# A two-layer graph kernel: self's first product issued inside the last round of left and right, with another order at the head and the end

## The chip, the cores and the metric

The kernel runs on one core of a Trainium2 chip. Times are device microseconds of one execution; the time of a kernel is the median of its runs. TensorE (PE in the profile) multiplies and transposes, VectorE (DVE) and ScalarE (ACT) work element by element and empty PE's banks, GpSimd (POOL) adds and issues stores, SyncE (SP) issues loads. Each engine works through its own queue in order and waits on semaphores of the others. A DMA is issued by an engine's queue and runs on 16 shared DMA engines.

## The reference

Inputs are x (128 graphs of 64 nodes, 768 features), one 64 x 64 adjacency for each graph and the weights of two layers, all in float32.

```python
# layer 0
p = softmax(h @ h.T / sqrt(768)); delta = p * adj
attn = delta / (delta.sum(2) + 1e-10)
ctx = upper(attn) @ (h @ Wl.T + bl) + diag(attn) * (h @ Ws.T + bs) + lower(attn) @ (h @ Wr.T + br)
x = layernorm(x + relu(layernorm(ctx, 1e-12) * gamma + beta))
# layer 1, 12 heads of 64
s = q @ k.T / sqrt(64) + beta * adj, masked where adj == 0
x = layernorm(x + softmax(s) @ v)
```

## The kernel before, in words

The 8192 tokens are worked through in 16 blocks (`NBLK`) of 512 tokens, four tiles of 128 (`T`). In the loop over n, layer 1 of block n runs interleaved with layer 0 of block m = n + 1, so that PE always has a product to issue. One turn of the loop goes through these stages on PE: left and right of block m, self of block m, its context, the values of block n, and q and k of block n in two groups.

**The products.** Left, right and self are 768 x 768 products done by a seven-product scheme (`seven`, numbered 1 to 7 in the order `ORDER` = 1, 2, 6, 5, 7, 4, 3): products 1, 6, 7 and 4 build in one PSUM bank (X), 2, 5 and 3 in another (Y), twice over for two token halves j. From block 3 on (`DEEP`) left and right are one nested scheme (`both_sides`, `nested`): seven rounds of seven products, weights from the DRAM tensor `lr_d` in tiles `wlr`. The next round's products 1 and 2 are issued ahead of a round's products 4 and 3; the last round has none after it, so there 4 follows 7 directly. DVE or ACT empties each bank into `u_deep` or `lr` (`middle` and `final`, L599, L601). Values, q and k use 15 products of 256-wide weights (`products`, L486), whose results DVE or ACT adds to `v` (L976) and `qk` (L1003, L1006). The banks X and Y are two each.

**Hooks.** Each stage calls `hooks.get(place)` before a product. `at(hooks, place, f)` puts work there: `sides` (four transposes into `ps_a`, L745, of the masked attention) at place 13 of the right hooks, `scores` and `weighted` of layer 1, loads, and `finish`. Element-wise work of other stages stands in three queues, `first`, `urgent` and `lazy`, and `step` issues one item after each product. So the order of each engine's instructions is fixed by places and queues when the program is built.

**The head.** Weights are first combined. `prepare1` makes 15 further forms of Wv (into `v_d`), Wq and Wk (`qk_d`): it loads nine pieces (L270, on SP's queue), forms 15 sums on DVE (`SUMS_W`, L303 and L305, one per step) and stores the forms that are multiplied (POOL's queue, L277, L284, L286). Pieces and sums live in a few buffers, `homes` (ten named `h_v`, eleven named `h_qk`), taken from the front of a list and put at its end when their last use is issued. Block 0 to 2 have plain left and right products (`side_part`), since `lr_d` is not ready. `deepened(i)` forms the second-level matrices of `lr_d` for one i: four loads into `w_deep` (four of the twelve buffers of the weight stream `wv`, `wqk`, `wl`), four copies from DRAM to DRAM, eight subtractions on DVE (L388), four stores (L394). A list gives the stage and place of each of the seven.

**The end.** `finish(p, lazy)` normalises block 14 inside the last block's q and k: sums and sums of squares by ACT (L1147, L1150), their variance by DVE (L1123), the root by ACT, the scaled tiles by ACT, stores by POOL. After the last value products come `sixth` parts of the weighted values of the last block (reciprocal and product on DVE, L1392 and L1393, adds on POOL or DVE, L1398), `bn_stats` and `bn_aggr` (L1409, L1412), and the four output tiles, three scaled by ACT and one by DVE, stored by SP (L1424, L1461).

Of the kernel before, what the change touches and what calls it, by code (L numbers as in the profile page):

```python
# [70 lines left out]
def gnn_two_layers(ctx: ExitStack, tc, x, adj, wl, bl, ws, bs, wr, br, gamma, beta,  # L71
# [174 lines left out]
    def prepare1(nm, homes, queue=lazy):  # L246

        w = weights[nm].rearrange("(p c) e -> p c e", c=KC)
        form, key = {}, ("w", nm)
        holder, done = {}, [0]  # L250

        def fresh_form(i):
            home = homes.pop(0)
            holder[i] = home
            return home.rearrange("p (k e) -> p k e", k=2)
# [6 lines left out]
        def loaded(i):  # L262
            if i in form:
                return
            k, j = divmod(i, THIRDS)
            form[i] = raw = fresh_form(i)
            if nm != "v":
                form[i] = raw.rearrange("p k (m e) -> p m k e", m=GROUPS)
            with tc.issue_after(streamed["l"][8] if nm == "k" else streamed["b", "r"].ins) if nm != "q" else ExitStack():
                nc.sync.dma_start(out=raw, in_=w[:, 2 * k : 2 * k + 2, j * TH : (j + 1) * TH])  # L270

# [16 lines left out]
        def summed(i, a, b, op):  # L288
            for _, *pair, _ in SUMS_W[done[0] : done[0] + AHEAD + 1]:
                for x in pair:  # L290
                    if x < THIRDS * THIRDS:
                        loaded(x)
            done[0] += 1
            fresh = [x for x in (a, b) if x < THIRDS * THIRDS and x not in known]
            known.update(fresh)
            form[i] = fresh_form(i)
            if nm != "v":
                form[i] = form[i].rearrange("p m (k e) -> p m k e", k=2)
            with tc.issue_after(recent["u"].ins) if nm == "v" else ExitStack():
                if op == "n":  # L300
                    parts = [form] if nm == "v" else [{k: form[k][:, m] for k in (i, a, b)} for m in range(GROUPS)]
                    for f in parts:
                        nc.vector.scalar_tensor_tensor(f[i], f[a], -1.0, f[b], ALU.mult, ALU.subtract)  # L303
                else:
                    nc.vector.tensor_tensor(form[i], form[a], form[b], ALU.add if op == "+" else ALU.subtract)  # L305
            for x in fresh:
                stored(x)
            stored(i)
            for x in (i, a, b):
                if x in uses:  # L310
                    uses[x] -= x != i
                if not uses.get(x):
                    homes.append(holder.pop(x))

# [212 lines left out]

    def seven(width, factors, first, last, hooks, taps_by_act=False):

# [6 lines left out]
        for k, i in enumerate(ORDER):  # L536
            for j in range(2):
                for f in hooks.get(2 * k + j, ()):
                    f()
                if i == 1:  # L540
                    X[j] = ps_st.tile([P, 512], F32, tag="X", name="ps_X")
                if i in (2, 5):
                    Y[j] = ps_st.tile([P, 512], F32, tag="Y", name="ps_Y")
                ps = (X if i in (1, 6, 7, 4) else Y)[j][:, 0:width]
                fs = factors(i, j)
                for c, (a, b) in enumerate(fs):
# [13 lines left out]
                elif i == 3:  # L560
                    last(j, 0, 1, ps, u[j, 2])
                step(not taps_by_act or (i, j) not in ((5, 1), (7, 0)))

    def by_tokens(nm, S, last, in_sbuf=None, hooks={}):

        wt = dict(in_sbuf or {})

        def factors(i, j):
# [11 lines left out]

        seven(HALF, factors, first, lambda j, m, n, ps, part: last(2 * m + j, n, ps, part), hooks)

# [168 lines left out]
    def self_part(n, in_sbuf, hooks={}):  # L751

        blk = blocks[n]
        o = [x1_p.tile([P, D], F32, tag="x1", name=f"o_{n}_{t}") for t in range(T)]

        def last(t, h, ps, part):
            cols = slice(h * HALF, (h + 1) * HALF)
            recent["u"] = nc.vector.tensor_tensor(o[t][:, cols], ps, bias["s"][:, cols] if part is None else part,
                                                  ALU.add)

        by_tokens("s", blk["S"], last, in_sbuf, hooks)
        blk["x"] = o
# [81 lines left out]
    def context0(n):  # L844
# [5 lines left out]
        if by_act:  # L850
            total, nm, var, std, rstd = (st.tile([P, T], F32, tag=f"c{k}", name=f"c{k}") for k in range(5))

        def unused():
# [57 lines left out]
        def norm(t, mean, rstd):  # L911
            if by_act and (n < NBLK - 1 or t % 2 == 0):
                nc.scalar.activation(o[t], o[t], AF.Identity, bias=nm[:, t : t + 1], scale=rstd)
            else:
                nc.vector.tensor_scalar(o[t], o[t], mean, rstd, ALU.subtract, ALU.mult)
# [7 lines left out]
        def rest(factors):  # L923
            for t, mr in enumerate(factors):
# [3 lines left out]
            fs = [partial(norm, t, *mr) for t, mr in enumerate(mrs)]  # L928
            later(key, *((tiny(partial(lowered, mrs)), *(f if n == NBLK - 1 and t % 2 else act(f) for t, f in enumerate(fs))) if by_act else
                         (lambda: (fs[0](), fs[1]()), lambda: (fs[2](), fs[3]()))))  # L930

# [173 lines left out]
    def finish(n, queue=urgent):  # L1105
# [5 lines left out]
        def sums(fs):  # L1111
            if ends:
                unused = l0t.tile([P, 2, 2, D], F32, tag="lr", name="unused")[:, 0, 0, :]
            else:
                unused = l1s_p.tile([P, T * 6 * L], F32, tag="s", name="unused")[:, 0:D]
            for t in range(T):
# [22 lines left out]

        def act(f):  # L1140
            return f, "root" if ends else "act"

        settle(("y", n, 0))
# [8 lines left out]

        if ends:

            begin = (summed, "after"), GAP, (lambda: (mean(), squared()), "act"), GAP, GAP, tiny(variance), act(root),                 GAP, GAP, GAP, tiny(factors)
        else:
            begin = (summed, "after"), GAP, GAP, tiny(mean), act(squared), GAP, GAP, tiny(variance), act(root), GAP,                 tiny(factors)
        later(key, *begin, *[act(partial(norm, (k, k + 1))) for k in range(0, T, 2)],
# [8 lines left out]
    edges(0)  # L1167
    homes = list(homes_of_v())
    now(loads(0))
# [28 lines left out]
    prep = streams.enter_context(tc.tile_pool(name="prep1", bufs=11))  # L1198
    homes = [prep.tile([P, 2 * TH], F32, tag="h", name="h_qk") for _ in range(11)]
    now(context0(0)[0])  # L1200
# [34 lines left out]
    for n in range(NBLK):  # L1235
# [11 lines left out]

        for i, (when, hooks, place) in zip(ORDER2, ((0, val, 2), (0, val, 8), (0, qk[0], 4), (0, qk[0], 10),
                                                    (0, qk[1], 6), (1, own, 3), (1, val, 3))):
            if when == n:  # L1250
# [8 lines left out]
        if p >= 0:  # L1259
# [141 lines left out]

    def behind(*parts):
        for h, j in parts:
            divided, added = sixth(h, j)
            later(("q", h, j), partial(divided, 0), lambda divided=divided, added=added: (
                divided(1), added(0, nc.gpsimd), added(1, nc.gpsimd)), queue=first)

# [14 lines left out]
    def norm_by_act(t):  # L1422
        nc.scalar.activation(xt[t], xt[t], AF.Identity, bias=shift[:, t], scale=rstd[:, t])
        nc.sync.dma_start(out=out_t[n, t], in_=xt[t])  # L1424

    def early():
# [7 lines left out]
    freed()  # L1434
    divided(0)
    divided(1)
    added(0, nc.gpsimd)
    added(1, nc.vector)
    divided, added = sixth(0, 2)
    for t in (2, 3):  # L1440
        measured(t, 0)
    for t in (0, 1):
        measured(t, 1)
    for t in (3, 2):
        measured(t, 1)
        whole(t)
    factors(slice(2, 4))
    divided(0)
    inverse(slice(2, 4))
    for t in (3, 2):  # L1450
        norm_by_act(t)
    divided(1)
    added(1, nc.gpsimd)
    added(0, nc.vector)
    for t in (0, 1):
        measured(t, 2)
        whole(t)
# [3 lines left out]
    nc.sync.dma_start(out=out_t[n, 0], in_=xt[0])  # L1461
    norm_by_act(1)
# [31 lines left out]
```

## Time and profile before

| | |
|---|---|
| median of 3 runs | 2823.55 us (2822.14 to 2825.18) |
| the profiled execution | 2829.61 us, span 2827.9 us |
| PE busy | 2783.3 us of the span, 17962 instructions |
| DVE, ACT, POOL busy | 1955.9, 1101.6, 958.5 us |
| mean granted clock of PE | 0.997 |
| PE and DVE busy from 100 to 200 us | 95.1 and 81.7 us, DMA share 0.76 |
| PE and DVE busy from 200 to 300 us | 95.1 and 78.9 us, DMA share 0.81 |

In a line of the timeline the columns are start, duration, engine, line of the kernel, operation, tiles written and read, partitions x elements, and how many instructions were drawn together; the bracket gives the idle time before and what ended it. One matmul of the source is two of them.

### The profile page before, as it was taken

The numbers are of one execution on the slowest core, as the hardware profiler recorded it, in microseconds if no ns is written. First come the engines' busy times: TensorE is split into PE (matmuls) and PEld (weight loads), VectorE is DVE, ScalarE is ACT, GpSimd is POOL, SyncE is SP. The second block draws the span as 40 slices with busy tenths as digits, with TensorE's granted clock in tenths as the row PEclk, the third lists the DMA queues.
The fourth block names the chain that finished last, engine by engine and source line by source line (L and its number), as shares of the span: only waits on it lengthen the run. The fifth ranks groups of instructions, "written<-read, shape, count | busy, mean of one in ns | idle before, by whom it ended". The sixth has DMA issues, their size and how long they took to land.

```text
span 2827.9 us, 49388 instructions
## 1 busy us (share of the span) xinstructions
PE 2783.3 (98%) x17962; PEld 2015.5 (71%) x17962; DVE 1955.9 (69%) x3399; ACT 1101.6 (39%) x1907; POOL 958.5 (34%) x1249
## 2 busy tenths in 40 slices
PE   9999999999999999999999999999999999999997
PEld 5558668686776867768577685867768677685786
DVE  5687777677685766767677676776767667676665
ACT  0003324435343452434525344353434534345255
POOL 3244232506134151442415225061341514424121
PEclk9999999999999999999999999999999999999998
DMA  9688595867869587695867858677695876958543
GB/s 345 196 283 271 179 306 171 265 157 232 223 184 272 145 261 193 190 267 152 260 183 211 246 168 264 161 231 226 184 266 147 258 198 192 266 147 260 172 124 98
DMA packets 394847, 604.87 MB, mean 214 GB/s; under 512 B 49296, under 2 KB 277648, under 8 KB 394608
## 3 DMA queue, kind: packets, MB, share of 16 engines
q1 hardware_dynamic: 344624, 502.80, 60.4%
q0 software_dynamic: 18704, 76.89, 7.5%
q10 hardware_dynamic: 31280, 22.03, 4.2%
q8 instruction: 145, 2.38, 0.4%
q14 instruction: 94, 0.77, 0.1%
HBM read 530.00 MB, written 78.45 MB: 215 GB/s over the span
## 4 chain that ended last, share of the span: by engine, by line
PE 87%; DVE 2%; DMA 2%; ACT 1%; issue 0%; DVEq 0%; ACTq 0%; SPq 0%
PE ps_X L486 25%; PE ps_Y L486 17%; PE ps_Y L816 13%; PE ps_X L816 11%; PE ps_X L547 8%; PE ps_Y L547 6%; PE ps_ctx L864 3%; PE sc L1027 2%; PE ps_y L1090 2%; PE u L694 1%; ACT eT L1060 1%; DMA wv<-v_d 0%; DMA sq<-in_x_dram 0%; DMA wlr<-lr_d 0%; DMA ws<-d_s 0%
## 5 line engine op out<-in xcount | busy, mean ns | idle before, releaser
L434 POOL TENSOR_TENSOR sums<-hT 128x768 f32<-128x768 f32 x16 | 28.9, 1808 | 828.2 <-PE ps_X L486 811.3
L1060 ACT ACTIVATE eT<-s 32x384 f32<-32x384 f32 x512 | 266.6, 521 | 44.0 <-DVE s L1043 37.6
L486 PE MATMUL ps_X<-xT,wqk 128*128 128x256 f32 x1024 | 236.2, 381 | 4.9 <-DVE qk L1006 2.5
L875 ACT ACTIVATE unused<-o 128x768 f32<-128x768 f32 x60 | 50.6, 843 | 477.4 <-DMA sq<-in_x_dram 261.1
L486 PEld LDWEIGHTS ps_X<-xT,wqk 128*128 128x128 f32 x1024 | 195.3, 191 | 32.7 <-DVE qk L1006 2.9
L601 DVE TENSOR_TENSOR lr<-ps_Y,u_deep 128x384 f32<-128x384 f32 x273 | 151.8, 556 | 95.8 <-PE ps_Y L816 78.8
L1003 ACT ACTIVATE qk<-ps_X,bq 128x256 f32<-128x256 f32 x128 | 60.6, 473 | 392.9 <-PE ps_X L486 392.7
L816 PE MATMUL ps_Y<-wlr,q 128*128 128x384 f32 x546 | 208.7, 491 | 0.0
L1006 DVE TENSOR_TENSOR qk<-qk,ps_X 128x512 f32<-128x512 f32 x160 | 109.6, 686 | 133.6 <-PE ps_X L486 73.7
L1101 POOL TENSOR_TENSOR o<-o,share 128x192 f32<-128x192 f32 x240 | 135.3, 591 | 145.3 <-DVE share L1098 145.2
L486 PE MATMUL ps_Y<-more,wqk 128*128 128x256 f32 x768 | 181.5, 379 | 0.2 <-DVE qk L1006 0.2
L486 PE MATMUL ps_X<-sums,wqk 128*128 128x256 f32 x768 | 180.3, 381 | 0.4 <-issue 0.4
L547 PE MATMUL ps_X<-ws,hT 128*128 128x384 f32 x540 | 179.4, 486 | 0.3 <-DMA ws<-d_s 0.3
L464 POOL TENSOR_TENSOR more<-xT 128x512 f32<-128x512 f32 x32 | 40.0, 1270 | 381.4 <-DVE xT L422 157.4
L486 PEld LDWEIGHTS ps_Y<-more,wqk 128*128 128x128 f32 x768 | 145.9, 190 | 20.4 <-DVE qk L1006 0.6
L486 PEld LDWEIGHTS ps_X<-sums,wqk 128*128 128x128 f32 x768 | 144.6, 190 | 20.7 <-issue 0.7
L1006 DVE TENSOR_TENSOR qk<-qk,ps_Y 128x512 f32<-128x512 f32 x160 | 108.2, 676 | 69.3 <-PE ps_Y L486 67.2
L601 DVE TENSOR_TENSOR u_deep<-ps_X,lr 128x384 f32<-128x384 f32 x195 | 107.6, 552 | 67.4 <-PE ps_X L816 58.0
L547 PEld LDWEIGHTS ps_X<-ws,hT 128*128 128x128 f32 x540 | 102.4, 190 | 72.0 <-DMA ws<-d_s 1.1
L816 PEld LDWEIGHTS ps_Y<-wlr,q 128*128 128x128 f32 x546 | 101.5, 190 | 67.5 <-DVE lr L601 0.5
L816 PE MATMUL ps_X<-wlr,q 128*128 128x384 f32 x364 | 149.1, 491 | 0.1
L1147 ACT ACTIVATE unused<-o 128x768 f32<-128x768 f32 x60 | 50.6, 844 | 219.2 <-POOL o L1101 216.3
(268 smaller groups left out, 6298.1 us busy)
## 6 DMA issues: line engine op xcount, KB each, us to landing
wlr<-lr_d SPq DMA_DIRECT2D x819, 192.0 KB, 3.6
wqk<-qk_d SPq DMA_DIRECT2D x480, 256.0 KB, 2.6
wv<-v_d SPq DMA_DIRECT2D x240, 256.0 KB, 5.6
ws<-d_s SPq DMA_DIRECT2D x180, 192.0 KB, 6.8
ws<-in_L_gnn_W_self_dram SPq DMA_DIRECT2D x135, 192.0 KB, 3.8
xa<-in_x_dram SPq DMA_DIRECT2D x64, 384.0 KB, 5.7
out_dram<-o POOLq DMA_DIRECT2D x60, 384.0 KB, 7.7
sq<-in_x_dram ACTq DMA_DIRECT2D x56, 384.0 KB, 9.7
```

The source lines that it names most:

```text
L486: nc.tensor.matmul(ps[:, h, :], lhsT=a, rhs=b, start=start and h == 0 and k == 0, stop=k == len(fs[h]) - 1, skip_group_check=True)
L547: nc.tensor.matmul(ps, lhsT=a, rhs=b, start=(c == 0 and i in (1, 2, 5)), stop=(c == len(fs) - 1), skip_group_check=True)
L601: nc.vector.tensor_tensor(dst, view(ps), add, ALU.add)
L816: nc.tensor.matmul(ps, lhsT=a, rhs=b, start=(k == 0 and j in (1, 2, 5)), stop=(k == len(fs) - 1), skip_group_check=True)
L864: nc.tensor.matmul(ps[g * L : (g + 1) * L, 0:HALF], lhsT=blk["aT"][:, t, g * L : (g + 1) * L], rhs=blk["lr"][t][:, g, h * HALF : (h + 1) * ...
L875: nc.scalar.activation(unused(), o[t], AF.Identity, accum_out=total[:, t : t + 1])
L1003: nc.scalar.activation(dst[:, h], ps[:, h, :], AF.Identity, bias=bias["qk"[h]][:, c : c + 1], scale=float(sign))
L1006: nc.vector.tensor_tensor(dst, dst, ps, ALU.add if sign > 0 else ALU.subtract)
L1027: nc.tensor.matmul(sc[t // 2, r][g * L : (g + 1) * L, t % 2, c, :], lhsT=q[rows, c, tok], rhs=k[rows, c, tok], start=True, stop=True)
L1060: nc.scalar.activation(e[to[0], :, to[1]], pairs[rows, :, cols], AF.Exp, scale=1.0 / SCALE)
L1090: nc.tensor.matmul(y[h, r][cols, t, c, :], lhsT=eT[rows, 2 * h + t, c, cols], rhs=by_parity[rows, 2 * h + t, 2 * c + m, g, :], start=True, ...
L1101: nc.gpsimd.tensor_tensor(res, res, share[:, t], ALU.add)
```

## The change

- Self's first product for token half 0 (three matmuls of the source and its three `ws` loads) is issued by `self_begun` at place 13 of the right hooks, right after `sides`, for blocks 3 to 15. Place 13 lies between products 7 and 4 of the last round. `seven` then skips that product in self's own stage and uses the begun bank.
- At the head, raw pieces are loaded by ACT's queue instead of SP's, homes are taken by age of release (with four steps added for a form that is stored), block 0's tiles are normalised by ACT, and the seven `deepened` get other places. Block 1's second `weighted` goes one product later.
- At the end, block 14's moments are taken by DVE's `bn_stats`, two of its tiles are scaled by DVE and two by ACT; the sixths are divided and added at once, all adds by POOL; the last block's tiles 2 and 0 are scaled by DVE, 3 and 1 by ACT.

```diff
         def fresh_form(i):
-            home = homes.pop(0)
-            holder[i] = home
+            home = min(homes, key=lambda h: h[0])
+            homes.remove(home)
+            holder[i] = home = home[1]
             return home.rearrange("p (k e) -> p k e", k=2)
...
-                nc.sync.dma_start(out=raw, in_=w[:, 2 * k : 2 * k + 2, j * TH : (j + 1) * TH])
+                nc.scalar.dma_start(out=raw, in_=w[:, 2 * k : 2 * k + 2, j * TH : (j + 1) * TH])
...
-                    homes.append(holder.pop(x))
+                    homes.append((done[0] + base + (4 if any(u == x for _, u, _, _ in FIFTEEN) else 0), holder.pop(x)))
...
+                ready = i == 1 and j == 0 and begun is not None
                 if i == 1:
-                    X[j] = ps_st.tile([P, 512], F32, tag="X", name="ps_X")
+                    X[j] = begun if ready else ps_st.tile([P, 512], F32, tag="X", name="ps_X")
...
-                fs = factors(i, j)
+                fs = [] if ready else factors(i, j)
...
+    def self_begun(n):
+
+        S = blocks[n]["S"]
+        w = [weight("ws") for _ in range(HC)]
+        ps = ps_st.tile([P, 512], F32, tag="X", name="ps_X")
+        for k in range(HC):
+            nc.sync.dma_start(out=w[k], in_=pieces["s"][1][:, k, :])
+        for k in range(HC):
+            nc.tensor.matmul(ps[:, 0:HALF], lhsT=S[1][:, k, 0:P], rhs=w[k], start=k == 0, stop=k == HC - 1,
+                             skip_group_check=True)
+        blocks[n]["begun"] = w, ps
...
         def norm(t, mean, rstd):
-            if by_act and (n < NBLK - 1 or t % 2 == 0):
+            if n < NBLK - 1 or t % 2 == 0:
...
         if ends:
-
-            begin = (summed, "after"), GAP, (lambda: (mean(), squared()), "act"), GAP, GAP, tiny(variance), act(root),                 GAP, GAP, GAP, tiny(factors)
...
+            mrs = moments(key, xt, 1e-5, queue)
...
+            later(key, tiny(lowered), (partial(by_act, 1), "root"), partial(by_vector, 0), (partial(stored, (0, 1)), "free"),
+                  (partial(by_act, 3), "root"), partial(by_vector, 2), (partial(stored, (2, 3)), "free"), queue=queue)
+            return
...
-        for i, (when, hooks, place) in zip(ORDER2, ((0, val, 2), (0, val, 8), (0, qk[0], 4), (0, qk[0], 10),
-                                                    (0, qk[1], 6), (1, own, 3), (1, val, 3))):
+        for i, (when, hooks, place) in zip(ORDER2, ((0, val, 2), (0, qk[0], 5), (1, left, 8), (1, own, 3),
+                                                    (1, qk[0], 0), (1, qk[0], 7), (1, qk[1], 3))):
...
-                at(right, 0 if m >= DEEP else 1, weighted, p, 1)
+                at(right, 0 if m >= DEEP else 2, weighted, p, 1)
...
                 at(*((left, 11) if m < DEEP else (right, 13)), sides, m)
+                if m >= DEEP:
+                    at(right, 13, self_begun, m)
...
-        at(qk[1], 5 if n == NBLK - 2 else 1, scores, n, 0)
+        at(qk[1], 4 if n == NBLK - 2 else 1, scores, n, 0)
         if last:
-            at(qk[1], 8, finish, p, lazy)
+            at(qk[1], 7, finish, p, lazy)
...
-    def behind(*parts):
...
+    def at_once(*parts):
+        for divided, added in [sixth(h, j) for h, j in parts]:
+            divided(0)
+            divided(1)
+            added(0, nc.gpsimd)
+            added(1, nc.gpsimd)
...
-               11: [partial(behind, (1, 2), (0, 0))], 13: [freed], 14: [early, partial(behind, (0, 1), (1, 0))]}, True)
+               11: [partial(at_once, (1, 2), (0, 0))], 12: [early], 14: [partial(at_once, (0, 1), (1, 0))]}, True)
...
     divided(0)
     divided(1)
     added(0, nc.gpsimd)
-    added(1, nc.vector)
+    added(1, nc.gpsimd)
...
-    for t in (3, 2):
-        norm_by_act(t)
...
+    norm_by_act(3)
+    measured(1, 2)
+    whole(0)
+    whole(1)
     factors(slice(0, 2))
+    norm_by_vector(2)
     inverse(slice(0, 2))
-    nc.vector.tensor_scalar(xt[0], xt[0], mv[:, 0, 0:1], rstd[:, 0], ALU.subtract, ALU.mult)
-    nc.sync.dma_start(out=out_t[n, 0], in_=xt[0])
+    norm_by_vector(0)
     norm_by_act(1)
```

More of the change, by code (lines that the diff above doesn't have):

```diff
@@ L249, in prepare1 @@
         form, key = {}, ("w", nm)
-        holder, done = {}, [0]
+        holder, done, base = {}, [0], len(SUMS_W) * "vqk".index(nm)
         def fresh_form(i):
-            home = homes.pop(0)
-            holder[i] = home
+            home = min(homes, key=lambda h: h[0])
+            homes.remove(home)
+            holder[i] = home = home[1]
             return home.rearrange("p (k e) -> p k e", k=2)
@@ L526, in moments, with seven @@
         return [(mv[:, t, 0:1], rstd[:, t : t + 1]) for t in range(k)]
-    def seven(width, factors, first, last, hooks, taps_by_act=False):
+    def seven(width, factors, first, last, hooks, begun=None):
         X, Y, u = {}, {}, {}
@@ L561, in seven, with by_tokens @@
                     last(j, 0, 1, ps, u[j, 2])
-                step(not taps_by_act or (i, j) not in ((5, 1), (7, 0)))
-    def by_tokens(nm, S, last, in_sbuf=None, hooks={}):
+                step()
+    def by_tokens(nm, S, last, in_sbuf=None, hooks={}, begun=None):
         wt = dict(in_sbuf or {})
+        if begun:
+            wt[1], begun = begun
         def factors(i, j):
@@ L579, in first @@
             return u
-        seven(HALF, factors, first, lambda j, m, n, ps, part: last(2 * m + j, n, ps, part), hooks)
+        seven(HALF, factors, first, lambda j, m, n, ps, part: last(2 * m + j, n, ps, part), hooks, begun)
+    def self_begun(n):
[8 more added lines that the diff above has]
+        blocks[n]["begun"] = w, ps
     def nested(width, sums, load, multiply, view, C, bias0, bias1, hooks):
@@ L759, in last @@
                                                   ALU.add)
-        by_tokens("s", blk["S"], last, in_sbuf, hooks)
+        by_tokens("s", blk["S"], last, in_sbuf, hooks, blk.get("begun"))
         blk["x"] = o
@@ L851, in context0 @@
             total, nm, var, std, rstd = (st.tile([P, T], F32, tag=f"c{k}", name=f"c{k}") for k in range(5))
+        else:
+            nm = st.tile([P, T], F32, tag="c1", name="c1")
         def unused():
@@ L928, in rest @@
             fs = [partial(norm, t, *mr) for t, mr in enumerate(mrs)]
-            later(key, *((tiny(partial(lowered, mrs)), *(f if n == NBLK - 1 and t % 2 else act(f) for t, f in enumerate(fs))) if by_act else
-                         (lambda: (fs[0](), fs[1]()), lambda: (fs[2](), fs[3]()))))
+            later(key, tiny(partial(lowered, mrs)), *(f if n == NBLK - 1 and t % 2 else act(f) for t, f in enumerate(fs)))
         return [partial(part, t) for t in range(T)], (squares, roots, inverse)
@@ L1111, in sums @@
         def sums(fs):
[L1112 to L1115, printed above, removed]
+            unused = l1s_p.tile([P, T * 6 * L], F32, tag="s", name="unused")[:, 0:D]
             for t in range(T):
@@ L1138, in stored @@
                 nc.gpsimd.dma_start(out=out_t[n, t], in_=xt[t])
-        def act(f):
-            return f, "root" if ends else "act"
         settle(("y", n, 0))
@@ L1153, in finish, with lowered, by_vector, by_act @@
         if ends:
-            begin = (summed, "after"), GAP, (lambda: (mean(), squared()), "act"), GAP, GAP, tiny(variance), act(root),                 GAP, GAP, GAP, tiny(factors)
-        else:
-            begin = (summed, "after"), GAP, GAP, tiny(mean), act(squared), GAP, GAP, tiny(variance), act(root), GAP,                 tiny(factors)
+            mrs = moments(key, xt, 1e-5, queue)
+            def lowered():
+                for t in (1, 3):
+                    mean, inverse = mrs[t]
+                    nc.vector.scalar_tensor_tensor(shift[:, t : t + 1], mean, -1.0, inverse, ALU.mult, ALU.mult)
+            def by_vector(t):
+                nc.vector.tensor_scalar(xt[t], xt[t], *mrs[t], ALU.subtract, ALU.mult)
+            def by_act(t):
+                nc.scalar.activation(xt[t], xt[t], AF.Identity, bias=shift[:, t : t + 1], scale=mrs[t][1])
+            later(key, tiny(lowered), (partial(by_act, 1), "root"), partial(by_vector, 0), (partial(stored, (0, 1)), "free"),
+                  (partial(by_act, 3), "root"), partial(by_vector, 2), (partial(stored, (2, 3)), "free"), queue=queue)
+            return
+        begin = (summed, "after"), GAP, GAP, tiny(mean), act(squared), GAP, GAP, tiny(variance), act(root), GAP, tiny(factors)
         later(key, *begin, *[act(partial(norm, (k, k + 1))) for k in range(0, T, 2)],
@@ L1167, in gnn_two_layers @@
     edges(0)
-    homes = list(homes_of_v())
+    homes = [(-1, home) for home in homes_of_v()]
     now(loads(0))
@@ L1198, in gnn_two_layers @@
     prep = streams.enter_context(tc.tile_pool(name="prep1", bufs=11))
-    homes = [prep.tile([P, 2 * TH], F32, tag="h", name="h_qk") for _ in range(11)]
+    homes = [(-1, prep.tile([P, 2 * TH], F32, tag="h", name="h_qk")) for _ in range(11)]
     now(context0(0)[0])
@@ L1400, in sixth @@
         return divided, added
-    def behind(*parts):
[L1403 to L1406, printed above, removed]
+    def at_once(*parts):
[4 more added lines that the diff above has]
+            added(1, nc.gpsimd)
     def measured(t, j):
@@ L1424, in norm_by_act, with norm_by_vector @@
         nc.sync.dma_start(out=out_t[n, t], in_=xt[t])
+    def norm_by_vector(t):
+        nc.vector.tensor_scalar(xt[t], xt[t], mv[:, t, 0:1], rstd[:, t], ALU.subtract, ALU.mult)
+        nc.sync.dma_start(out=out_t[n, t], in_=xt[t])
     def early():
@@ L1430, in gnn_two_layers @@
     values(n, {1: [partial(scores, n, 1, 2, l0t, 7)],
-               11: [partial(behind, (1, 2), (0, 0))], 13: [freed], 14: [early, partial(behind, (0, 1), (1, 0))]}, True)
+               11: [partial(at_once, (1, 2), (0, 0))], 12: [early], 14: [partial(at_once, (0, 1), (1, 0))]}, True)
     settle(("f", n - 1))
     divided, added = sixth(1, 1, ps_st)
-    freed()
+    measured(0, 1)
+    measured(1, 1)
     divided(0)
@@ L1437, in gnn_two_layers @@
     added(0, nc.gpsimd)
-    added(1, nc.vector)
+    added(1, nc.gpsimd)
     divided, added = sixth(0, 2)
+    measured(2, 0)
+    measured(3, 0)
+    divided(0)
+    divided(1)
+    added(0, nc.gpsimd)
+    added(1, nc.gpsimd)
     for t in (2, 3):
-        measured(t, 0)
-    for t in (0, 1):
-        measured(t, 1)
-    for t in (3, 2):
         measured(t, 1)
@@ L1447, in gnn_two_layers @@
     factors(slice(2, 4))
-    divided(0)
+    measured(0, 2)
     inverse(slice(2, 4))
-    for t in (3, 2):
-        norm_by_act(t)
[L1452 to L1457, printed above, removed]
+    norm_by_act(3)
+    measured(1, 2)
+    whole(0)
+    whole(1)
     factors(slice(0, 2))
+    norm_by_vector(2)
     inverse(slice(0, 2))
-    nc.vector.tensor_scalar(xt[0], xt[0], mv[:, 0, 0:1], rstd[:, 0], ALU.subtract, ALU.mult)
-    nc.sync.dma_start(out=out_t[n, 0], in_=xt[0])
+    norm_by_vector(0)
     norm_by_act(1)
```

## The prediction

> **What bounds the kernel now.** I read the page first: its engine table, then its chain.
>
> ```profile
> PE 2783.3 (98%) x17962; PEld 2015.5 (71%) x17962; DVE 1955.9 (69%) x3399; ACT 1101.6 (39%) x1907; POOL 958.5 (34%) x1249
> ...
> PE 87%; DVE 2%; DMA 2%; ACT 1%; issue 0%; DVEq 0%; ACTq 0%; SPq 0%
> ```
>
> TensorE is the bound, idle 2827.9 − 2783.3 = 44.6 us. The change removes no matmul, so it can win only idle time, where the chain leaves PE. I next walked PE's timeline, taking each gap between starts beyond the usual spacing (0.32 us for 384 columns, 0.22 for 256) as lost. A sixth block, PE then DVE:
>
> ```profile
> 1391.54 0.60 PE L745 MATMUL ps_a<-ident,a 128*128 128x128 f32 x4
> 1392.35 1.56 PE L816 MATMUL ps_X<-wlr,sums 128*128 128x384 f32 x4 [0.21 <-DVE u_deep L601]
> 1393.74 1.46 PE L816 MATMUL ps_Y<-wlr,q 128*128 128x384 f32 x4
> 1395.04 3.39 PE L547 MATMUL ps_X<-ws,hT 128*128 128x384 f32 x10
> ...
> 1391.74 0.56 DVE L601 TENSOR_TENSOR u_deep<-ps_X,lr 128x384 f32<-128x384 f32 x1 [1.31 <-PE ps_X L816]
> ```
>
> After product 7 and four transposes, product 4 (1392.35) waits until DVE has emptied product 7's bank. From the last transpose to product 4 it is 0.486 us where 0.109 is usual; the next interval is 0.427 instead of 0.323. Lost: 0.377 + 0.104 = 0.48 us, the same in all 13 blocks that have this round. The head (first 420 us, PE and DVE):
>
> ```profile
> 92.01 2.20 PE L547 MATMUL ps_X<-t_r,hT 128*128 128x384 f32 x6 [1.76 <-DVE u L578]
> ...
> 90.80 0.69 DVE L305 TENSOR_TENSOR h_v<-h_v 128x512 f32<-128x512 f32 x1 [3.35 <-issue]
> ...
> 175.73 2.17 PE L547 MATMUL ps_Y<-wr,hT 128*128 128x384 f32 x6 [2.42 <-issue]
> ...
> 173.78 0.69 DVE L305 TENSOR_TENSOR h_qk<-h_qk 128x512 f32<-128x512 f32 x1 [4.25 <-DMA qk_d<-h_qk]
> ...
> 233.45 1.75 PE L486 MATMUL ps_X<-wv,sums 128*128 128x256 f32 x7 [1.97 <-DMA wv<-v_d]
> ...
> 268.42 1.75 PE L486 MATMUL ps_X<-xT,wqk 128*128 128x256 f32 x7 [2.00 <-DMA wqk<-qk_d]
> ```
>
> Two kinds: DVE, in order, stands before a weight sum whose buffer is still being stored, and evictions queue behind it; or a weight stream is late because one `deepened` holds four of its twelve buffers. The end:
>
> ```profile
> 2775.25 3.34 PE L486 MATMUL ps_X<-xT,wqk 128*128 128x256 f32 x7 [2.46 <-DVE qk L1006]
> ...
> 2774.43 0.17 DVE L1123 TENSOR_SCALAR f<-f 128x4 f32<-128x4 f32 x1 [3.69 <-ACT unused L1150]
> ...
> 2823.48 0.33 SPq L1461 DMA_DIRECT2D out_dram<-o  x1
> 2824.00 0.33 SPq L1424 DMA_DIRECT2D out_dram<-o  x1
> ```
>
> DVE waits 3.69 us for ScalarE's sums of squares while a q/k eviction stands behind; the seven matmuls after it take 3.34 us for 1.75, with a granted clock of 0.5 for 3.4 us.
>
> **The change, part by part.**
>
> *Self's first product.* Three matmuls (six instructions, 6 × 0.323 = 1.94 us) go between the transposes and product 4. They need a bank emptied long before (1388.78 + 0.56), so they start at once, and the eviction that product 4 waits for (it ends at 1392.30) lies under them. Gain 13 × 0.48 = 6.2 us. Their cover: the three `ws` loads keep their place on SP's queue and landed 4.4 to 8.9 us before first use; used 3.07 us earlier, the tightest third load (4.36, used 1.29 us into the product) keeps 2.6 us. Next late is self's second half, which takes the bank of product 4: that is empty 3 × 0.32 + 0.53 + 0.56 + 0.06 = 2.11 us after product 4 starts and wanted after 2.58 us, so 0.47 us remain. DVE's order there is unchanged; product 3's eviction and the ScalarE swaps (12 × 0.86 us) come 1.5 us later, first wanted at 1425.7.
>
> *Head: homes and ScalarE's queue.* Twenty-seven loads of v, q and k pieces leave SP's queue for ScalarE's, where hT copies, exponentials and square roots stand behind them; sums now take the longest-freed buffer. Value sum 14 gets a buffer with no store. Lost at 89.8 and 93.7: 2.03 + 0.54 = 2.6; I take 2.2, as one later sum may still wait. At 172.8 and 177.4: 2.66 + 1.12 = 3.8; q sum 22 now follows an early store, but the next k sum waits for a load (these took 3.0 to 6.8 us from issue to landing): 3.0, bounds 0 to 3.8. Five early loads (1.28 MB at 390 GB/s) delay the streams of left and right by 3.3 us; these landed 8.6 and 18 us before use, so nothing. Block 0's four norms (0.75 us each) go from DVE to ScalarE against four tiny scalings (0.17): 2.3 us off DVE, where 0.77 + 0.54 = 1.3 were lost at 192 to 195: 0.7. Norm 3 is queued behind a k load that waits for a store; stores of that stretch landed at 184 to 187, so the norm ends near 190, wanted at 201.
>
> *Head: `deepened`.* Block 0 keeps two of five; block 1 has five for two, three of them in its q/k stage. Lost now: 2.3 at 231, 2.4 at 266, 1.06 + 0.85 behind DVE at 298 and 302, 1.4 at 406: 8.0, of which 7.0 should go. The new three: none does worse than 2.4 (total 0 to 7.2); the five in block 0 cost (2.3 + 2.4 + 1.9)/5 = 1.3 each, the two in block 1 0.7; I take 1.0 each, −3.1. Block 1's second weighted sum moves one product later, but its eT transposes come after another eviction: −0.3.
>
> Head: 2.2 + 3.0 + 0.7 + 7.0 − 3.1 − 0.3 = 9.5.
>
> *End.* The moments of block 14 become eight `bn_stats` (0.43 to 0.51) and four aggregates (0.2) on DVE; no DVE instruction waits for a long ScalarE chain. Gone: 2.7 at 2772, 1.7 of half clock, 0.46 at 2770. Added: two runs of about 2.3 us on DVE, each with an eviction (0.68) in a 1.73 us product, less one bank of slack: up to 1.3 us late each; I take −1.6. That is 3.3. After the last value eviction (2811.3) DVE ran without a pause to 2823.45. From there go four divisions of 0.55, done earlier in its idle time, and two adds (0.90 + 0.42) to POOL; one norm (0.67) comes: −2.2 − 1.3 + 0.7 = −2.8. Next late is POOL's last add (0.72 to 0.96 each): 2.6, bounds 1.0 to 2.8. End: 5.9.
>
> A rule weighed here: in this trace one 2.42 us wait (175.73) was followed by matmuls at full speed (2.17 us for six), another of 2.46 by half clock, so a wait of that size does not decide alone. The Trainium skill ("TensorE: Matmul & The Clock Gate", "Why this matters for your kernels") puts the drop at idle gaps above about 3 us, seen through a free-running window; by that no wait here would suffice, and the 1.7 us would stay.
>
> **Sum.** 6.2 + 9.5 + 5.9 = 21.6. The profiled execution took 2829.6 (span 2827.9 and 1.7 around it): 2808.0. It was 6.1 above the median of the runs, so against 2823.55: 2802.
>
> **Rivals.**
> - *The head's waits only move.* For it: DVE is 82% busy from 100 to 200 us, DMA 81% from 200 to 300, and five `deepened` now meet in block 1. Against: of the two there now, one cost nothing. The head then gives 1.5: 2810.
> - *The begun product hands the wait on*, to self's second half: one 0.68 us DVE instruction ahead of product 4's eviction would outlast the 0.47 us. None is queued there. Steady gain nothing: 2808.
> - *The half clock stays*: whatever set it off was not the 2.46 us wait alone, and what idle is left there does it too; 1.7 less: 2804. With the `bn_stats` at their worst too: 2805. (2804 is what the page of the Trainium skill named above would give.)
> - *Slower: DVE starved of raw pieces.* q and k pieces on ScalarE's queue are issued only once the buffer ahead is stored. Fourteen pieces come after the first sum; one made DVE wait in the trace of before (1.02 us at 158.88). Price 14 × the mean wait, paid by PE since DVE is 82% busy there: it eats the whole gain from 1.5 us per piece and ends 0.2% slower from 1.9: 2829 and up. Against: pieces are asked for three sums ahead, and sums are about 2 us apart.
>
> **How the numbers follow.** Forecast 2802 with 0.62; head 0.15; handed on 0.06; clock or moments 0.08; starved 0.05; 0.04 for losses that cancel near zero. The range takes the forecast with every stall gone (block 1's three free, +3; end at its best, +2; homes +2: 2795) up to the head rival with a weaker end (2813). A measurement of this kernel tells about 0.2%, 5.6 us, from no change. All rivals but two keep the 6.2 or the head: faster 0.89, same 0.05, slower 0.06.
>
> **What would show it.** Right: in each of 13 blocks an L547-type product directly after the transposes at 0.11 us spacing and product 4 without a DVE wait; no PE gap above 1 us at about 90, 173, 231, 266, 406 and 2772; full clock to the last matmul; some 14 us from last matmul to end down to about 11.5. Wrong: a wait on DVE at self's second half 13 times; DVE waits on h_qk loads; wqk waits over 2 us in block 1's q/k stage; or a first value product later than before.

## The result and the profile after

The changed kernel takes 2814.04 us (median of 9 runs, 2812.4 to 2820.74); the kernel before, run beside it, 2823.94 us (9 runs, 2822.14 to 2825.18). The ratio is 0.9968, with a 95% interval of 0.9959 to 0.9976. The medians lie 9.9 us apart; 21.6 were forecast, and 2814.04 lies just above the range.

The page of the changed kernel, first the span, the engines and the chain that ended last:

```profile
span 2811.9 us, 49390 instructions
...
PE 2775.8 (99%) x17962; PEld 2014.2 (72%) x17962; DVE 1951.1 (69%) x3412; ACT 1099.0 (39%) x1894; POOL 961.5 (34%) x1251
...
PE 92%; issue 2%; DMA 2%; DVE 2%; ACT 1%; POOL 0%; SPq 0%; POOLq 0%; ACTq 0%; DVEq 0%
```

PE does the same 17962 instructions and idles 2811.9 − 2775.8 = 36.1 us, where it was 44.6. The two profiled executions lie 16.0 us apart, not 9.9: that of before took 5.7 us more than its kernel's median, that of after 0.4 less than its own.

PE's timeline of the changed kernel, the round in block 6 that the prediction showed:

```profile
1383.43 0.60 PE L761 MATMUL ps_a<-ident,a 128*128 128x128 f32 x4
1383.87 2.10 PE L595 MATMUL ps_X<-ws,hT 128*128 128x384 f32 x6
1385.81 1.45 PE L832 MATMUL ps_X<-wlr,sums 128*128 128x384 f32 x4
1387.10 1.45 PE L832 MATMUL ps_Y<-wlr,q 128*128 128x384 f32 x4
1388.39 2.10 PE L549 MATMUL ps_X<-ws,hT 128*128 128x384 f32 x6
```

Self's first product (L595) stands behind the four transposes. Product 4 follows it 1.94 us later, which is six times the 0.323 us of one matmul: no bracket, so no wait on DVE. Self's next product, half 1 (1388.39), does not wait either.

Aligning the two profiles matmul by matmul shows where the 16.0 us went (gains positive; a time called lost is the gap between two starts beyond the usual spacing, some 0.16 us more than the idle time in the bracket):

| stretch | us |
|---|---|
| start, and right's quarters near 55 us | 1.1 − 4.9 |
| values and right of blocks 0 and 1, to 205 us | 6.4 |
| block 0's values, q and k; block 1's left, self | 8.2 |
| block 1's values, q and k | −6.0 |
| 13 rounds, 0.48 each | 6.2 |
| three `wlr` loads that were late in the trace of before | 1.6 |
| the end, to the last matmul | 1.1 |
| after the last matmul | 2.2 |

The −4.9 is a loss that the prediction had put at nothing. DVE and PE of the changed kernel near 57 us, one fence for each engine:

```profile
57.04 0.56 DVE L355 TENSOR_TENSOR t_r<-b_r 128x384 f32<-128x384 f32 x1 [7.81 <-DMA b_r<-in_L_gnn_W_right_dram]
57.63 1.12 DVE L803 TENSOR_TENSOR lr<-ps_Y,u 64x384 f32<-64x384 f32 x2
```

```profile
53.71 2.10 PE L549 MATMUL ps_Y<-t_l,sums 128*128 128x384 f32 x6
58.90 3.78 PE L549 MATMUL ps_Y<-t_l,sums 128*128 128x384 f32 x6 [3.09 <-DVE lr L803]
```

DVE stood 7.81 us before the first sum of right's weights, and left's evictions (L803) behind it in its queue. PE wanted the bank that they empty. The six matmuls from 58.90 took 3.78 us where those from 53.71 took 2.10: the granted clock was 0.5 (half clock) from 59.3 to 62.7 us.

### The profile page after: what moved, and what is told of

The parts are those of the page before. It is cut to its first block, busy times and chain, and to the rows that moved or that the text cites. A ratio compares the mean times of both kernels' runs of the same rounds, so it can differ in the third digit from the quotient of the medians.

```text
span 2811.9 us, 49390 instructions
## 1 busy us (share of the span) xinstructions
PE 2775.8 (99%) x17962; PEld 2014.2 (72%) x17962; DVE 1951.1 (69%) x3412; ACT 1099.0 (39%) x1894; POOL 961.5 (34%) x1251
## 3 DMA queue, kind: packets, MB, share of 16 engines
q1 hardware_dynamic: 337280, 495.72, 59.3%
## 4 chain that ended last, share of the span: by engine, by line
PE 92%; issue 2%; DMA 2%; DVE 2%; ACT 1%; POOL 0%; SPq 0%; POOLq 0%; ACTq 0%; DVEq 0%
PE ps_X L487 25%; PE ps_Y L487 17%; PE ps_Y L832 13%; PE ps_X L832 11%; PE ps_X L549 10%; PE ps_Y L549 8%; PE ps_ctx L882 3%; PE sc L1044 2%; PE ps_y L1107 2%; PE u L710 1%; PE ps_X L595 1%; ACT eT L1077 1%; DMA b_r<-in_L_gnn_W_right_dram 1%; DMA qk_d<-h_qk 0%; DVE lr L803 0%
## 5 line engine op out<-in xcount | busy, mean ns | idle before, releaser
L549 PE MATMUL ps_X<-ws,hT 128*128 128x384 f32 x462 | 154.0, 486 | 0.0
L549 PEld LDWEIGHTS ps_X<-ws,hT 128*128 128x128 f32 x462 | 87.7, 190 | 61.0 <-DMA ws<-d_s 0.2
```

Source lines behind the costliest of these rows:

```text
L549: nc.tensor.matmul(ps, lhsT=a, rhs=b, start=(c == 0 and i in (1, 2, 5)), stop=(c == len(fs) - 1), skip_group_check=True)
```

## The experiments

The ratios in this section are against the kernel before on the same chip; the median of before was 2824.73, 2825.28 and 2824.64 us on the three chips used.

**v_sync: the pieces of Wv on SP's queue again.** Five of these loads are the early ones.

```diff
-                nc.scalar.dma_start(out=raw, in_=w[:, 2 * k : 2 * k + 2, j * TH : (j + 1) * TH])
+                (nc.sync if nm == "v" else nc.scalar).dma_start(out=raw, in_=w[:, 2 * k : 2 * k + 2, j * TH : (j + 1) * TH])
```

> The changed kernel, but Wv's nine pieces are loaded on SP's queue again (the homes stay by age). Theory: the five early v pieces on ScalarE's queue push right's quarters back, DVE stands in order before the sum t5_r until 57 us, left's evictions queue behind it, and PE loses 3.25 + 0.29 us and then 1.6 us of half clock. So the wait at 55 us and the half clock go: 5.1 less than the changed kernel, 2809. The wait at 90 us stays away, since the homes cure it. Rival, the queue itself is what cures the wait at 90: 2.4 comes back there, 2811.5. Rival, the half clock there is chance and not a consequence of the wait: only 3.5 less, 2810.5.

Measured: 2808.78 us (5 runs, 2807.18 to 2811.51), ratio 0.9942 (0.993 to 0.9955), an interval wholly below that of the changed kernel; once more on another chip it is 2809.8, with a wider interval (`v_sync_2`, below). DVE in this kernel:

```profile
50.72 0.56 DVE L355 TENSOR_TENSOR t_r<-b_r 128x384 f32<-128x384 f32 x1
```

The sum runs at 50.72, with no bracket, and the wait at 55 us and its half clock are gone. The waits near 90 us that the order of `homes` was to remove stay away too. So the wait near 55 us belongs to ScalarE's early loads, and the gain of the `homes` does not need them.

**late_sum: the loads as in the changed kernel, but right's sums later on DVE.** This tells apart whether the late quarters or DVE's order made PE wait.

```diff
-            with tc.issue_after(recent["u"].ins) if nm == "l" else ExitStack():
+            with tc.issue_after(recent["u"].ins) if nm in "lr" else ExitStack():
...
-    in_sbuf_r = prepare("r", prep, wst, (4, 0, 3))
+    in_sbuf_r = prepare("r", prep, wst, (8, 0, 0))
```

> The changed kernel, v's loads early on ScalarE's queue as there, but right's sums t5_r to t4_r are put on DVE behind left's evictions. Theory: not the late quarters cost the 5.1 us but that DVE, in order, stands before t5_r with evictions behind it; the quarters landed at 54 to 59 us, and right's own products need them from 70: 5.1 less, 2809, as with v's loads on SP. Rival, right's quarters are late for PE as well: the wait comes again at right's first products, 2812 or more.

Measured: 2810.26 us (5 runs, 2808.41 to 2814.11), ratio 0.9949 (0.9936 to 0.9961), an interval that just touches the changed kernel's. The four quarters landed as late as in the changed kernel (54.4 to 60.2 us; 53.8 to 59.6 there). DVE and PE of this kernel:

```profile
61.34 1.12 DVE L803 TENSOR_TENSOR lr<-ps_Y,u 64x384 f32<-64x384 f32 x2
62.49 1.49 DVE L355 TENSOR_TENSOR t_r<-b_r 128x384 f32<-128x384 f32 x3
```

```profile
54.74 4.03 PE L549 MATMUL ps_Y<-t_l,sums 128*128 128x384 f32 x12
58.61 4.03 PE L549 MATMUL ps_X<-b_l,hT 128*128 128x384 f32 x12
```

The sums now stand behind the eviction, and PE does 24 matmuls at the usual spacing. Late quarters alone cost PE nothing; a DVE instruction that waits for them ahead of an eviction does.

**no_begun and begun_only: self's product taken out of the changed kernel, and put alone into the kernel before** (there with the bank that `seven` then takes from it).

```diff
-                if m >= DEEP:
-                    at(right, 13, self_begun, m)
```

> The changed kernel without self's begun product. Theory: 13 times 0.48 us return, 2820.2, each between the transposes and product 4. Rival, the wait was only handed on inside the block (to self's second half or to the context): no change, 2814.

> The kernel before with self's begun product alone. Theory: 6.2 less than before, 2817.7, and head and end as before. If so the rest of the change is worth 3.7 in the median, though the two profiles differ there by 9.8. Rival, the product's gain hangs on the other parts: no change, 2824.

Measured: without it 2820.99 us (11 runs, 2817.85 to 2825.71), ratio 0.9986 (0.9977 to 0.9994); alone 2817.45 us (8 runs, 2814.5 to 2821.01), ratio 0.9974 (0.9964 to 0.9984). It is worth 7.0 us by the medians of the changed kernel without and with it (5.1 by the ratios), 7.3 added to the kernel before. The forecast was 6.2, which lies among these, and 13 × 0.48 is what the timeline shows. So head and end together were worth only some 3 of the 15.4 us forecast.

**old_deep: the changed kernel with the seven `deepened` at their old places.**

```diff
-        for i, (when, hooks, place) in zip(ORDER2, ((0, val, 2), (0, qk[0], 5), (1, left, 8), (1, own, 3),
-                                                    (1, qk[0], 0), (1, qk[0], 7), (1, qk[1], 3))):
+        for i, (when, hooks, place) in zip(ORDER2, ((0, val, 2), (0, val, 8), (0, qk[0], 4), (0, qk[0], 10),
+                                                    (0, qk[1], 6), (1, own, 3), (1, val, 3))):
```

> The changed kernel with the list of deepened of before (five in block 0, two in block 1). Theory: the three in block 1's q and k stage cost what the five in block 0 did, so the places are worth little: the waits near 403, 432, 473 and 480 us go (1.46 + 1.45 + 1.57 + 2.42 = 6.9) and those of before at 231, 266, 298, 302 and 407 return (8.4 with the small ones): 1.5 more than the changed kernel, 2815.5. Rival, the places are the change's main gain at the head: the four waits stay whatever the list, since other work makes them, and 8 is lost: 2822.

Measured: 2815.95 us (5 runs, 2812.57 to 2820.09), ratio 0.9962 (0.9949 to 0.9976), which overlaps the changed kernel's interval. The new places are worth 1.9 us by the medians and less than nothing by the ratios: no gain that these runs can tell, where 7.0 − 3.1 = 3.9 was forecast. In its profile nothing is lost near 473 and 480 us, and 2.50 is lost again at 236 us, as the expectation had it.

**old_tail: the changed kernel with the end of before** (the moments, that is means and variances, by ScalarE's sums, the old last chain and the old places; of the edit, the places are shown).

```diff
-        at(qk[1], 4 if n == NBLK - 2 else 1, scores, n, 0)
+        at(qk[1], 5 if n == NBLK - 2 else 1, scores, n, 0)
...
-            at(qk[1], 7, finish, p, lazy)
+            at(qk[1], 8, finish, p, lazy)
```

> The changed kernel with the end of before (block 14's sums on ScalarE and the old last chain and places). Theory: at the end most of what was won was given back (1.24 + 1.27 behind the moments, 0.96 before block 15's transposes, 1.35 before the first sixths), so the new end is worth the 1.1 + 2.2 that the profiles differ by: 3.3 more than the changed kernel, 2817.3. Rival, the new end is worth the 5.9 forecast and the profile of before hid it: 2820.

Measured: 2816.71 us (6 runs, 2815.38 to 2818.15), ratio 0.9972 (0.996 to 0.9984). By the medians the new end is worth 2.7 us, not 5.9; the intervals overlap.

**before_again: the kernel before, unedited**, for a second profile.

> The kernel before, profiled once more. Theory: its first profile was 5 us slower than its median by waits that are not there in most executions: the one at 266 us (2.16 and its neighbour), the DMA waits in the steady blocks (0.77 + 0.44 + 0.24) and 0.66 at the start; the waits near 90, 173, 231 and 2772 us and the half clock after the last are there again. Span about 2823. Rival, all of them are there again: 2828.

Measured: 2825.35 us, span 2823.6. PE in it:

```profile
260.69 1.89 PE L486 MATMUL ps_Y<-more,wqk 128*128 128x256 f32 x8
265.99 5.33 PE L486 MATMUL ps_X<-xT,wqk 128*128 128x256 f32 x16 [3.41 <-DMA wqk<-qk_d]
...
2771.07 3.62 PE L486 MATMUL ps_X<-xT,wqk 128*128 128x256 f32 x8 [2.46 <-DVE qk L1006]
```

The wait on DVE at the end is the same to the hundredth (2.46). The waits on loads are not: that at 266 us went from 2.16 lost to 3.57 and half clock, against the expectation; the 2.13 at 231 fell to 0.34; two of the three `wlr` waits are gone. The loss near 90 us, too, was 1.01 where it was 1.93. So the span came out near the 2823 expected, but not by the waits that were named. These waits moved by 0.9 to 1.8 us either way from one execution to the other, and the sum of the prediction took those of one execution as they were.

**spread: v_sync with the three `deepened` of block 1's q and k further apart.**

```diff
-        for i, (when, hooks, place) in zip(ORDER2, ((0, val, 2), (0, qk[0], 5), (1, left, 8), (1, own, 3),
-                                                    (1, qk[0], 0), (1, qk[0], 7), (1, qk[1], 3))):
+        for i, (when, hooks, place) in zip(ORDER2, ((0, val, 2), (0, qk[0], 5), (0, qk[1], 1), (1, left, 8),
+                                                    (1, own, 3), (1, qk[0], 4), (1, qk[1], 2))):
```

> v_sync (2808.8) with one of the three deepened of block 1's q and k stage moved to block 0's second q/k group, the others at places 4 and 2. Theory: three at once take steps from block 2's moments, which then stand in a row on DVE before the first round of left and right, and the ACT copy that PE waits for (2.4 us near 472, with half clock behind it in some runs) stands behind its norm; with two the moments are through in time: the waits near 428, 468 and 472 go, 3.5 less, 2805.3. Rival, the one moved costs 2.0 by DVE near 295 as it did in before: 2807.

Measured: 2809.31 us (5 runs, 2808.73 to 2811.59), ratio 0.9947 (0.9934 to 0.9959): no gain over v_sync. PE in this kernel, at the place where the changed kernel waits 2.25 us:

```profile
475.10 0.88 PE L832 MATMUL ps_X<-wlr,q 128*128 128x384 f32 x2 [0.51 <-issue]
```

The stall there is nearly gone, but new ones stand at 283 us (1.02) and 461 (0.54), both behind DVE's q/k evictions, and the loss near 470 us is 1.94 where v_sync had 1.55. This edit moved a cost.

**apart, both, v_sync_2.** `apart` is v_sync with block 14's `bn_stats` one tile for each product, and the first sixths one product later; `both` has these two edits on top of spread; `v_sync_2` is v_sync once more, on the same chip.

```diff
-        later(key, *[partial(one, t) for t in range(k - 1)], last_one,
+        later(key, *[f for t in range(k - 1) for f in (partial(one, t), *([GAP] if apart else []))], last_one,
...
-               11: [partial(at_once, (1, 2), (0, 0))], 12: [early], 14: [partial(at_once, (0, 1), (1, 0))]}, True)
+               12: [partial(at_once, (1, 2), (0, 0))], 13: [early], 14: [partial(at_once, (0, 1), (1, 0))]}, True)
```

> v_sync (2808.8) with block 14's moments one tile per product instead of two, and the first sixths one product later. Theory: the two waits of 1.22 and 1.26 us behind the moments are the four tiles standing in two pairs on DVE, and the sixths wait for an exponential chain that did not get shorter: with both undone 2.3 and 1.3 less, 2805.2. Rival, the moments end later and the norms after them make the next stage wait as long: 2808 or more.

> spread (2809.3, in its profile 2.0 below that of v_sync) with the same two edits at the end. Theory: the end's 3.6 us come on top: 2805.7. Rival as for apart: 2809.

> v_sync again, on the same chip as the two others, so that they can be compared with it. Theory: 2808.8, its ratio to the kernel before 0.994 again; the half clock behind the 2.4 us wait near 472, there in its first profile and not in that of the changed kernel, may be there or not.

Measured: apart 2809.65 us (5 runs, 2805.19 to 2812.82), ratio 0.9945 (0.9932 to 0.9957); both 2807.07 us (5 runs, 2805.18 to 2810.46), 0.9939 (0.9926 to 0.9951); v_sync_2 2809.8 us (5 runs, 2807.24 to 2817.06), 0.9949 (0.9935 to 0.9963). PE of apart at the two places where the changed kernel waits 1.08 and 1.10 us on q/k evictions (shown in the next section):

```profile
2757.39 1.89 PE L487 MATMUL ps_X<-more,wqk 128*128 128x256 f32 x8
2759.21 1.99 PE L487 MATMUL ps_X<-sums,wqk 128*128 128x256 f32 x8
2761.04 1.89 PE L487 MATMUL ps_Y<-more,wqk 128*128 128x256 f32 x8
```

Both waits are gone, so a run of `bn_stats` was their cause. The median of apart did not follow: for its time the experiment is inconclusive. What may hide it is a loss near 402 us that differs between executions: 2.73 in apart's profile, none in v_sync's, and in v_sync_2's this:

```profile
405.35 3.00 PE L487 MATMUL ps_X<-wv,more 128*128 128x256 f32 x8 [3.85 <-issue]
```

DVE waited there for an x load (`sq`, 6.55 us in v_sync_2, 4.01 in the changed kernel) with evictions behind it. `both` is the fastest version of all; its interval lies below the changed kernel's and overlaps v_sync's, so of its 7 us over the changed kernel only what v_sync brings is told apart.

## Why the prediction was wrong, and where it was right

**Right: self's first product.** 6.2 us from 0.48 in each of 13 blocks; every round shows it, no wait is handed on to self's second half, and the runs give 7.0 (5.1 by the ratios) and 7.3. The rival "handed on" did not occur.

**Right: homes, block 0's norms and the old `deepened` waits.** The forecast 2.2 + 3.0 + 0.7 = 5.9 measured 6.4, and the 7.0 of waits that should go measured 8.4. That the first sum agrees better than its parts is luck: 2.3 near 90 us, 1.9 near 175, 1.3 near 194 and 0.9 in places without a term. Near 167 us DVE still stands 2.50 us before a sum of q or k for a store (4.25 before). Still, the rival "the head's waits only move" is what the head came close to: 3.7 us are left of it (that rival had 1.5), because of the next two points.

**Wrong: "landed 8.6 and 18 us before use, so nothing".** This is the step that failed most plainly: 0 forecast, −4.9 in the profile; taking the loads back brought 5.3 us by the medians, 4.2 in `v_sync_2`. Two things in this step were wrong. The delay was more than the 3.3 us worked out: the first quarter landed at 42.4 us before and at 53.8 after, the third at 48.6 and 56.95. And the word "use" took the use on PE. Right's quarters are used first by DVE's sums, and DVE had left's evictions behind them. In the trace of before:

```profile
50.36 0.56 DVE L354 TENSOR_TENSOR t_r<-b_r 128x384 f32<-128x384 f32 x1
51.14 1.12 DVE L787 TENSOR_TENSOR lr<-ps_Y,u 64x384 f32<-64x384 f32 x2 [0.22 <-PE ps_Y L547]
```

The sum ran there without a wait, 1.8 us after the third quarter; in the changed kernel it ran at 57.04, just after that quarter. So the slack was to be read on the in-order engine that touches the data first: 1.8 us, not 18. The loss needed the larger delay as well. By an estimate from these rows, a sum that started 3.25 us earlier (53.8) would have cost PE nothing, and with a delay of 3.3 us the third quarter would have landed at 51.9. Why five loads delayed the quarters by 7 to 11 us and not by 3.3, no run shows.

**Wrong in size: the new `deepened` at 1.0 each.** −3.1 was forecast with a bound of −7.2, and −7.1 measured. Five losses in block 1's values, q and k make it up (1.46, 1.45, 1.57, 2.42 and 0.17). Only the second is a late weight stream, the kind that the price came from. The first is DVE's wait for an x load, and in other kernels with the same places the loss there was 0 to 4.01, so it can't be laid to the places. The third and fourth, 4.0 together, stand in all seven kernels with these places to 0.02 us each, and not in old_deep. DVE, then ACT, around the largest, which ends at 480.03 on PE:

```profile
471.10 1.01 DVE L517 BATCH_NORM_STATS2 stats<-o 128x6 f32<-128x384 f32 x2
...
472.82 1.83 DVE L1081 STREAM_TRANSPOSE eT<-eT 128x768 f32<-128x768 f32 x2
```

```profile
477.89 0.21 ACT L525 ACTIVATE std<-std 128x4 f32<-128x4 f32 x1 [4.91 <-DVE std L522]
...
478.54 1.03 ACT L931 ACTIVATE o<-o,c,rstd 128x768 f32<-128x768 f32 x1 [0.44 <-DVE c L927]
479.47 0.46 ACT L615 COPY u_deep<-ps_X 128x384 f32<-128x384 f32 x1
```

The weight sums in the same queues moved block 2's moments to where exponentials are transposed; ACT's root waits 4.91 us for DVE's variance, and the copy that empties PE's bank waits behind root and norm. Moving a `deepened` moves the queue items around it, and these were not followed.

**Wrong in size, with two terms missing: the end.** "I take −1.6" measured −2.5 (1.24 and 1.27 behind the moments), and two losses without a term took 2.3 more: 0.96 before block 15's transposes and 1.35 before the first sixths. The q/k products of block 15 on PE:

```profile
2757.57 1.99 PE L487 MATMUL ps_X<-sums,wqk 128*128 128x256 f32 x8 [1.08 <-DVE qk L1023]
2760.67 1.99 PE L487 MATMUL ps_Y<-more,wqk 128*128 128x256 f32 x8 [1.10 <-DVE qk L1023]
```

These two are the "up to 1.3 us late each" that the prediction worked out and then cut from 2.6 to 1.6. The others come from the order on ScalarE. With `scores` one product earlier (place 4 for 5), two norms of 1.03 us stand among sixteen exponentials, where one of the two had stood ahead of them: the copies that PE's transposes wait for begin 10.55 us after the first exponential, and 9.57 before. In old_tail it is 9.58, and the loss is back at 0.54. Ahead of the first sixths a table load moved. ScalarE in the trace of before, then in the changed kernel:

```profile
2780.51 1.28 ACT L1060 ACT_TABLE_LOAD   x1
2789.55 8.53 ACT L1060 ACTIVATE eT<-s 32x384 f32<-32x384 f32 x16 [7.76 <-DVE s L1043]
```

```profile
2775.05 1.28 ACT L1077 ACT_TABLE_LOAD   x1 [11.33 <-DVE s L1060]
2776.35 8.55 ACT L1077 ACTIVATE eT<-s 32x384 f32<-32x384 f32 x16
```

Before, the load of 1.28 us ran in idle time, 9 us ahead of the exponentials; now it starts only when DVE's scores are ready, the exponentials end that much later, and PE waits 1.39 us for their result (at 2786.91). All four profiles with the old end have the first order (old_tail too), and all nine with the new end the second; which part of the new end sets it, no run tells apart. What was to go did go: no wait of 2.46 on a q/k eviction, and full clock behind it.

**Right: the last chain.** 2.6 forecast, 2.2 measured; 14.0 us from the last matmul to the end of the span became 11.8. SP's stores in the changed kernel:

```profile
2806.03 1.07 SPq L1455 DMA_DIRECT2D out_dram<-o  x2
2807.25 0.66 SPq L1451 DMA_DIRECT2D out_dram<-o  x1
```

**The balance.** Put against the table, self gave its 6.2; the head gave 6.4 + 8.2 − 6.0 − 4.9 = 3.7 for 9.5; the end gave 1.1 + 2.2 = 3.3 for 5.9. That is 13.2 for 21.6: 8.4 of the 11.7 us that the forecast was too high by are its own terms. The profiles differ by 2.7 more (start 1.1, late `wlr` loads 1.6) that no edit explains, and by 6.1 less once each is set against its kernel's median; 13.2 + 2.7 − 6.1 = 9.8, the measured 9.9 but for rounding. So the other 3.3 us are put down to chance: waits were counted from one execution that ran 5.7 us long and were carried to the median whole, and a second profile of before has 4.3 us less span with nothing edited. Which of the counted waits these were stays open.

**The rival on the slower side** did not occur: no wait of DVE for the load of a q or k piece reached PE.

## What to carry to other kernels

Read the slack of a load at the first instruction that touches it on any in-order engine, and ask what is queued behind that instruction; PE's own first use came 20 us later here. When a wait is cured by moving a step, follow every queue item that the step displaces, and price the worst place, not the mean. Take waits on transfers from at least two executions: between the two of before, losses by an engine's order came back to 0.01 us (2.62 and 2.62, 1.37 and 1.37), those by loads 1.4 to 1.8 us differently, and one in v_sync's two profiles by 4.0.

## What the runs showed of the hardware

After a wait PE's granted clock was sometimes 0.5, for 3.4 us in most cases and for 6.8 after the two longest waits. The waits are given here as time lost. All six above 3 us in these profiles were followed by it (3.25, 3.28, 3.57, 4.01, 4.37 and 6.06 us). Of fifteen between 2.4 and 2.75 us, eleven were and four were not. Of six between 1.9 and 2.2, one was: 1.95 us in the kernel `both`, with a clock of 0.5 from 470.7 to 474.1 us, while 1.94 us at the same matmul in spread was not. Once a shorter one was, 1.37 us and then 0.7 in begun_only (0.5 from 332.8 us). One wait of 2.41 us shows either outcome. The changed kernel and v_sync, on PE:

```profile
480.03 0.88 PE L832 MATMUL ps_X<-wlr,q 128*128 128x384 f32 x2 [2.25 <-issue]
...
481.39 1.45 PE L832 MATMUL ps_Y<-wlr,hT 128*128 128x384 f32 x4
```

```profile
474.96 0.88 PE L832 MATMUL ps_X<-wlr,q 128*128 128x384 f32 x2 [2.25 <-issue]
...
476.68 2.77 PE L832 MATMUL ps_Y<-wlr,hT 128*128 128x384 f32 x4
```

Four matmuls after an equal idle time take 1.45 us in one and 2.77 in the other; behind the second, the whole stretch lost 1.7 us. The Trainium skill ("TensorE: Matmul & The Clock Gate", "Why this matters for your kernels") warns of gaps above about 3 us; the traces agree above 3 us, but idle times of 2.24 to 2.57 us were enough in most cases, and 1.79 once. The same page tells of a free-running window (Part 1); that equal waits end both ways fits it, and no run here tested it. The wait at the end of before (2.62) was followed by half clock in all four profiles that have it, and with the wait the half clock went: the forecast's 1.7 us there were right, and the rival that would have kept them was not.
